# Mixer projections of groups 1 to 7 as 2x2 block products in one fixed order, with the first convolution tap on ScalarE

## Chip, cores and metric

The kernel runs on one core of one Trainium2 chip. The metric is the device time of one execution in microseconds (us), taken as the median of several runs; the profile is of one further execution. All data are float32.

## What is computed

The reference is one decoder block on `x` of 8 sequences with 64 tokens each (512 tokens, 512 channels): a layer norm and a cross-attention (32 heads, 8 key/value heads, 1601 context rows per sequence), a layer norm and a state-space mixer, a layer norm and a routed low-rank expert stage, each added to `x`. The change touches the mixer:

```python
proj = jnp.einsum('bld,pd->blp', hidden_states, in_proj_w)
gate = proj[..., :I]; hbc = proj[..., I:I + CONV_DIM]; dt = proj[..., -H:]
pad = jnp.pad(hbc, ((0, 0), (K - 1, 0), (0, 0)))
conv = conv_bias
for k in range(K):                                   # K = 4 taps
    conv = conv + pad[:, k:k + L, :] * conv_weight[:, k]
xBC = jax.nn.silu(conv)                              # x, B and C
dt_p = jax.nn.softplus(dt + dt_bias); dA = jnp.exp(-dt_p * jnp.exp(A_log))
# scan over tokens: state = state * dA + dt_p * x (outer) B;  y = state . C
y = jnp.moveaxis(ys, 0, 1) + x * D[None, None, :, None]
yg = y.reshape(B, L, G, GROUP_SIZE)
yn = yg * lax.rsqrt(jnp.mean(yg * yg, -1, keepdims=True) + EPS) * norm_weight * silu(gate)
out = jnp.einsum('bli,di->bld', yn, out_proj_w)
```

## The kernel before

The kernel works through the attention first (to about 2268 us of the span), then `mixer_and_routed`, in which the mixer's 64 heads are taken as 8 groups of 8 heads. A group's weights `w_in` make ten row tiles n of 128 rows: n = 0 to 3 are the gates, 4 to 7 the heads' x, 8 is B, 9 is C. Group 0 makes all ten with `project` (L1213 to L1223): four 128x512 matmuls per tile over the contraction of 512, in one PSUM bank `pj`. A float32 matmul leaves two records in the trace, so a tile is 8 records of line L1217. Groups 1 to 7 make tiles 4 to 9 with `project`, and the gates as two pairs of tiles, (0, 1) and (2, 3), with `project_gates` (L1268): a pair of tiles by two halves of 512 channels by two halves of 512 tokens is a 2x2 block product, made with seven half-size products in place of eight.

```python
FIRST = (("a", "L11", "R11"), ("d", "S2", "T2"), ("b", "S1", "T1"), ("c", "S3", "T3"))
SECOND = (("a", "L12", "R21"), ("b", "S4", "R22"), ("c", "L22", "T4"))
```

`first()` makes four of them into the banks `pj_ab` and `pj_cd` (16 records of 128x256, L1279), after which ScalarE copies `a` (L1294) and VectorE makes three sums (L1296 to L1298); `second()` accumulates the other three (12 records) and leaves two more sums (L1305, L1306). The weight sums S1 to S4 come from GpSimd (`weight_sums`, L161 to L164; four instructions per pair, tile `ws`), the token sums T1 to T4 once from VectorE (L1148).

For tiles 4 to 9, `project` goes on with the convolution: the first tap with the bias from PSUM (L1228, VectorE), three more taps (L1234, VectorE, reading `pj` in PSUM and adding to `acc` in SBUF), SiLU (L1240 or L1242, ScalarE). x is also scaled by D (L1246), transposed in 32x32 blocks (L1249, VectorE), and turned by four stores to DRAM (`x_d`) on SyncE's queue and four loads by `load_x` (`dx`).

The other steps, by the names that the change and the trace use: `steps` (L1178, GpSimd, `av`) and `decay` (32 records of L1201 into `seg`, then four Exp into `dec`, L1207) make the decays of a group. `mix` makes C·B (L1317, `pg`), masks it (L1322, `gm`), multiplies it into the decays (L1329, `m`, VectorE) and scales `dx` by dt (L1332, GpSimd). `scan` makes the outputs of a group (128 records of L1347, `py`) and adds them to `y` (L1353, VectorE). `gate` makes the squares (`sq`, ScalarE and GpSimd) and multiplies `y` by the gates (L1369, VectorE). `norm` sums the squares (L1375, `pss`), `project_out` makes the output projection of one of four blocks of 128 tokens (8 records of L1387, `mo`) and adds it to `x` (L1391, VectorE).

A group's decays, scan, gates, norm and outputs run one group late (`old`), between the projections of the group `G`; the decays of the next group (`new`) come a group ahead. The main loop (L1460 on) gives the order in which steps are issued, with `tc.issue_after` at the places where order matters; a list scheduler and the pools settle the rest. The pools are stacked in SBUF in the order in which they are opened: `grpp` (decays, gates, B and C), then `wst` (the weights `w_in` and `w_out`, two buffers each), then `big` and `wk`. `load_in(groups[0])` issues the first group's weights (L1063: four DMAs, two of 1 MB and two of 256 KB) on SyncE's queue while the attention still runs; its address decides which earlier tile has to be free first.

## Time and profile before

| | us |
|---|---|
| median of 3 runs | 2722.01 |
| lowest and highest of them | 2721.52, 2722.79 |
| profiled execution, own time | 2723.19 |
| its span | 2721.5 |
| of the span, TensorE busy | 2703.6 (99%) |
| VectorE, ScalarE, GpSimd busy | 1754.3, 788.8, 802.9 |
| from the mixer's first projection (2272.86) to the end | 448.6 |

The profiled execution's own time is 1.7 us more than its span, and 1.2 us more than the median. In the views, times are microseconds from the start of the span, PE is TensorE's matmuls, PEld its weight loads, DVE VectorE, ACT ScalarE, POOL GpSimd and SP SyncE; "x8" is the number of records in a row, and what stands in brackets is how long the engine had waited and for whom.

### The profile page before, as it was taken

Reading aid. Unit: us, or ns where it says so; the run is one execution under the profiler, and the core shown is the slowest. Engines: PE = TensorE matmul, PEld = TensorE weight load, DVE = VectorE, ACT = ScalarE, POOL = GpSimd, SP = SyncE. Lnnn points to the kernel's source line nnn. Section 1 sums busy time; section 2 is a strip of 40 time slices with the busy share of each in tenths; the row PEclk is TensorE's granted clock in tenths of the full one; section 3 lists DMA queues with packets and bytes.
Section 4 is the critical chain, followed back from the end, with each engine's and each line's share of the span. In section 5 each row is a group of like instructions: output and inputs, shape, how many; then the busy total and the mean of one; then the engine's idle time right before and its main releaser. Section 6 shows DMA issues by size and latency. Waiting matters only on the chain.

```text
span 2721.5 us, 39370 instructions
## 1 busy us (share of the span) xinstructions
PE 2703.6 (99%) x15218; PEld 2002.0 (74%) x15218; DVE 1754.3 (64%) x3071; ACT 788.8 (29%) x1386; POOL 802.9 (30%) x810
## 2 busy tenths in 40 slices
PE   9999999999999999999999999999999999999998
PEld 8777787877788777778787777887777654555555
DVE  5666676576667666766666676667666425676576
ACT  3322222222222232222222222222322102434433
POOL 5323223222222223322333222222333221433321
PEclk9999999999999999999999999999999999999999
DMA  5921322131223213222322132123212370534431
GB/s 174 303 73 48 83 66 62 49 106 44 51 56 90 57 40 79 83 59 42 81 75 61 40 106 50 45 55 92 55 40 71 108 243 12 144 89 107 115 84 41
DMA packets 349716, 222.87 MB, mean 82 GB/s; under 512 B 223932, under 2 KB 309050, under 8 KB 348506
## 3 DMA queue, kind: packets, MB, share of 16 engines
q1 hardware_dynamic: 349530, 220.36, 29.7%
q8 instruction: 121, 1.98, 0.3%
q14 instruction: 65, 0.53, 0.1%
HBM read 189.26 MB, written 31.05 MB: 81 GB/s over the span
## 4 chain that ended last, share of the span: by engine, by line
PE 89%; DVE 6%; DMA 2%; issue 1%; ACT 0%; POOL 0%; SPq 0%; DVEq 0%; ACTq 0%; POOLq 0%
PE pav L647 13%; PE psc L577 13%; PE pv_a L494 6%; PE pv_b L494 6%; PE pk_b L431 6%; PE pk_c L431 6%; PE pv_c L494 6%; PE pk_a L431 6%; PE mo L1387 4%; PE pj L1217 3%; PE pv_d L494 3%; PE pk_d L431 3%; DVE acc L1234 2%; PE psn L463 2%; PE pj_cd L1279 1%; PE pq_ab L241 1%
## 5 line engine op out<-in xcount | busy, mean ns | idle before, releaser
L582 DVE SCALAR_TENSOR_TENSOR attn<-psc,rk,mask_sb 128x256 f32<-128x256 f32 (+1 forms) x832 | 364.5, 476 | 201.2 <-PE psc L577 196.5
L631 POOL TENSOR_TENSOR sm<-attn 128x512 f32<-128x512 f32 x64 | 81.9, 1279 | 1188.3 <-ACT attn L629 1188.3
L647 PE MATMUL pav<-attn,v 128*128 128x256 f32 (+1 forms) x1664 | 380.5, 379 | 0.4 <-ACT o L663 0.4
L577 PE MATMUL psc<-q,kT 128*128 128x256 f32 x1536 | 367.1, 380 | 0.0
L634 POOL TENSOR_TENSOR sm<-sm,attn 128x512 f32<-128x512 f32 x256 | 339.5, 1326 | 29.6 <-DVE attn L625 10.4
L577 PEld LDWEIGHTS psc<-q,kT 128*128 128x128 f32 x1536 | 287.6, 190 | 76.3 <-issue 28.6
L647 PEld LDWEIGHTS pav<-attn,v 128*128 128x128 f32 (+1 forms) x1664 | 311.5, 190 | 43.0 <-issue 1.0
L625 DVE TENSOR_TENSOR attn<-attn,nb 128x1024 f32<-128x1024 f32 x192 | 225.0, 1216 | 52.4 <-ACT nb L622 52.4
L629 ACT ACTIVATE attn<-attn 128x1024 f32<-128x1024 f32 x192 | 203.1, 1058 | 77.7 <-DVE attn L625 71.8
L593 DVE TENSOR_TENSOR mx<-mx,attn 128x512 f32<-128x512 f32 x256 | 212.1, 829 | 2.0
L494 PEld LDWEIGHTS pv_a<-wv,cx 128*128 128x128 f32 x1536 | 191.4, 192 | 9.2 <-issue 2.4
L494 PE MATMUL pv_a<-wv,cx 128*128 128x128 f32 x1536 | 197.9, 275 | 0.0
L431 PE MATMUL pk_a<-cx,wk 128*128 128x417 f32 (+1 forms) x512 | 193.3, 500 | 0.2 <-DVE q_raw L275 0.2
L1217 PE MATMUL pj<-mx_xnT,w_in 128*128 128x512 f32 x416 | 184.8, 597 | 0.0
L442 ACT ACTIVATE ksq<-kT 128x834 f32<-128x834 f32 (+1 forms) x128 | 109.2, 871 | 144.2 <-DVE kT L423 144.2
L1217 PEld LDWEIGHTS pj<-mx_xnT,w_in 128*128 128x128 f32 x416 | 77.1, 190 | 91.9 <-issue 89.3
L431 PEld LDWEIGHTS pk_a<-cx,wk 128*128 128x128 f32 x512 | 97.2, 190 | 45.5 <-issue 21.9
L1387 PE MATMUL mo<-w_out,y 128*128 128x512 f32 x256 | 115.3, 592 | 0.0
L622 ACT COPY nb<-nbs 128x256 f32<-128x256 f32 x64 | 24.1, 376 | 295.6 <-DMA nbs<-max_d 254.6
L421 ACT COPY kT<-pk_a 128x384 f32<-128x384 f32 x64 | 31.5, 493 | 267.4 <-PE pk_a L431 267.4
L694 POOL TENSOR_TENSOR o<-o,f 128x512 f32<-128x512 f32 x31 | 39.7, 1281 | 220.1 <-DMA f<-sums_d 181.9
L1234 DVE SCALAR_TENSOR_TENSOR acc<-pj,small_consts,acc 128x504 f32<-128x504 f32 (+1 forms) x144 | 102.7, 727 | 3.0
(249 smaller groups left out, 4364.1 us busy)
## 6 DMA issues: line engine op xcount, KB each, us to landing
wk<-in_wk SPq DMA_DIRECT2D x32, 512.0 KB
wv<-in_wv SPq DMA_DIRECT2D x32, 512.0 KB
w_in<-in_w_in SPq DMA_DIRECT2D x16, 1024.0 KB
wvs<-wv_s_d SPq DMA_DIRECT2D x28, 512.0 KB
wks<-wk_s_d SPq DMA_DIRECT2D x28, 512.0 KB
cx<-in_ctxT SPq DMA_DIRECT2D x16, 834.0 KB
cx<-in_ctxT SPq DMA_DIRECT2D x16, 768.0 KB
wq<-in_wq SPq DMA_DIRECT2D x16, 512.0 KB
```

The costliest lines, as they stand in the source:

```text
L431: nc.tensor.matmul(ps[:, :w], lhsT=u.wk[l][:, dc, :], rhs=u.cx.r[ch][r][:, dc, :], start=start and dc == 0, stop=dc == 1, skip_group_check ...
L494: nc.tensor.matmul(ps[:, i * HD : (i + 1) * HD], lhsT=u.cx.r[ch][r][:, dc, i * P : (i + 1) * P], rhs=u.wv[l][:, dc, :], start=start and i ...
L577: nc.tensor.matmul(ps[:rows, t - t2, :], lhsT=lhsT, rhs=qh, start=True, stop=True)
L582: nc.vector.scalar_tensor_tensor(out=s.at[:rows, t, :].rearrange("p (h q) -> p h q", h=GQ), in0=ps[:rows, t - t2, :].rearrange("p (h q) -> ...
L593: nc.vector.tensor_tensor(s.mx2, s.mx2, s.at[:, t2 : t2 + 2, :], ALU.max)
L625: nc.vector.tensor_tensor(at[:, k : k + 4, :], at[:, k : k + 4, :], nb.unsqueeze(1).to_broadcast([P, 4, 256]), ALU.add,)
L629: nc.scalar.activation(at[:, k : k + 4, :], at[:, k : k + 4, :], AF.Exp)
L634: nc.gpsimd.tensor_tensor(sm2, sm2, at[:, i : i + 2, :], ALU.add)
L647: nc.tensor.matmul(s.av[:, 0, :], lhsT=u.v[:rows, t, hh, :], rhs=s.at[:rows, t, :], start=t == 0, stop=t == NKT - 1,)
L1217: done = nc.tensor.matmul(pj, lhsT=G.w[:, dc, n, :], rhs=xnT[:, dc, :], start=dc == 0, stop=dc == DC - 1).ins
L1234: taps = nc.vector.scalar_tensor_tensor(out=accb[:, :, k:], in0=pjb[:, :, : S - k], scalar=c.cw[:, ct, KC - 1 - k : KC - k], in1=accb[:, : ...
L1387: last = nc.tensor.matmul(po, lhsT=G.y[:, n, tt * P : (tt + 1) * P], rhs=G.wo[:, n, :], start=n == 0, stop=n == GC - 1,)
```

## The change

All five pairs of tiles, (4, 5), (6, 7), (8, 9), (0, 1) and (2, 3), of groups 1 to 7 go through `project_pair`, the former `project_gates` (names X1, X2, X0, Z0, Z1). The x, B and C pairs are put together in a new SBUF tile `xin`; `convolve` then reads `xin`, with its first tap and bias on ScalarE (Identity with scale and bias) and the other three taps on VectorE. Group 0 keeps `project`, in another order of tiles. The main loop becomes one chain of TensorE steps: each `pe(...)` is issued behind the step before it. PSUM's `pj` has 4 banks in place of 3; the bank `px` is gone, and layer norms and outputs use `y0`, `y1` or `seg`. In SBUF `dec` and `bc` have one buffer in place of two, `p1` and `u2` two in place of one, `ws` four in place of two, and `xin` two.

The diff, without the lines of the old main loop and with smaller hunks left out:

```diff
     def bank(tag, shape, name, bufs=1):
-        return (ps4 if tag in ("pj", "y1") else ps).tile(shape, F32, tag=tag, name=name, bufs=bufs)
+        return (ps4 if tag == "pj" else ps).tile(shape, F32, tag=tag, name=name, bufs=bufs)
...
-        G.l[n] = weight_sums(nc, l, wk.tile([P, 4, 2, P], F32, tag="ws", name="ws"))
+        G.l[n] = weight_sums(nc, l, wk.tile([P, 4, 2, P], F32, tag="ws", name="ws", bufs=4))
...
-                nc, c, small, ps, x, tt, xnT[:, :, tok], tag="px", bufs=2, pbufs=1, copy=nc.scalar.copy
+                nc, c, small, ps, x, tt, xnT[:, :, tok], tag="y0", bufs=2, pbufs=1, copy=nc.scalar.copy
...
-        G.dec = grpp.tile([P, NTT, HPG, S], F32, tag="dec", name="dec")
+        G.dec = grpp.tile([P, NTT, HPG, S], F32, tag="dec", name="dec", bufs=1)
...
-        return last.ins
+        G.exps = last.ins
+        return done.ins
...
-        pj = bank("pj", [P, NT], "pj", 3)
+        pj = bank("pj", [P, NT], "pj", 4)
...
+        return done, convolve(G, n, pj, True), None
+
+    def convolve(G, n, pj, taps):
...
-            G.bc = grpp.tile([P, 2, NT], F32, tag="bc", name="bc")
+            G.bc = grpp.tile([P, 2, NT], F32, tag="bc", name="bc", bufs=1)
...
-        nc.vector.tensor_scalar(
-            acc, pj, c.cw[:, ct, KC - 1 : KC], c.cb[:, ct : ct + 1], op0=ALU.mult, op1=ALU.add
-        )
+        if taps:
+            nc.vector.tensor_scalar(
+                acc, pj, c.cw[:, ct, KC - 1 : KC], c.cb[:, ct : ct + 1], op0=ALU.mult, op1=ALU.add
+            )
+        else:
+            nc.scalar.activation(
+                acc, pj, AF.Identity, scale=c.cw[:, ct, KC - 1 : KC], bias=c.cb[:, ct : ct + 1]
+            )
         accb = acc.rearrange("p (b t) -> p b t", b=B)
         pjb = pj.rearrange("p (b t) -> p b t", b=B)
         for k in range(1, KC):
-            taps = nc.vector.scalar_tensor_tensor(
+            nc.vector.scalar_tensor_tensor(
                 out=accb[:, :, k:], in0=pjb[:, :, : S - k],
                 scalar=c.cw[:, ct, KC - 1 - k : KC - k], in1=accb[:, :, k:],
                 op0=ALU.mult, op1=ALU.add,
...
-    def project_gates(G, n):
+    def project_pair(G, n):
         st, l = Group(), G.l[n]
-        if n == 0:
-            G.sg = grpp.tile([P, GC, NT], F32, tag="sg", name="sg")
-        to = G.sg[:, n : n + 2]
+        gates = n < GC
...
+            if n == 0:
+                G.sg = grpp.tile([P, GC, NT], F32, tag="sg", name="sg")
+            st.to = G.sg[:, n : n + 2] if gates else wk.tile([P, 2, NT], F32, tag="xin", name="xin")
             st.ps = {}
             for pair in ("ab", "cd"):
-                t = bank("pj", [P, 2, HT], f"pj_{pair}", 3)
+                t = bank("pj", [P, 2, HT], f"pj_{pair}", 4)
                 st.ps[pair[0]], st.ps[pair[1]] = t[:, 0, :], t[:, 1, :]
             for k, lhs, rhs in FIRST:
...
-            p1 = wk.tile([P, HT], F32, tag="p1", name="p1", bufs=1)
+            p1 = wk.tile([P, HT], F32, tag="p1", name="p1")
             nc.scalar.copy(p1, st.ps["a"])
-            st.u2 = wk.tile([P, HT], F32, tag="u2", name="u2", bufs=1)
+            st.u2 = wk.tile([P, HT], F32, tag="u2", name="u2")
             nc.vector.tensor_tensor(st.u2, p1, st.ps["d"], ALU.add)
             nc.vector.tensor_tensor(p1, st.u2, st.ps["b"], ALU.add)
-            nc.vector.tensor_tensor(to[:, 1, HT:], p1, st.ps["c"], ALU.add)
+            nc.vector.tensor_tensor(st.to[:, 1, HT:], p1, st.ps["c"], ALU.add)
             return last
         def second():
+            to = st.to
             for k, lhs, rhs in SECOND:
                 last = product(k, lhs, rhs, False, True)
-            nc.scalar.activation(to[:, 0, :HT], st.ps["a"], AF.Silu)
+            if gates:
+                nc.scalar.activation(to[:, 0, :HT], st.ps["a"], AF.Silu)
+            else:
+                nc.scalar.copy(to[:, 0, :HT], st.ps["a"])
             nc.vector.tensor_tensor(to[:, 0, HT:], st.u2, st.ps["b"], ALU.add)
             nc.vector.tensor_tensor(to[:, 1, :HT], st.u2, st.ps["c"], ALU.add)
-            nc.scalar.activation(to[:, 0, HT:], to[:, 0, HT:], AF.Silu)
-            return last, nc.scalar.activation(to[:, 1, :], to[:, 1, :], AF.Silu).ins
-
-        return first, second
+            if gates:
+                nc.scalar.activation(to[:, 0, HT:], to[:, 0, HT:], AF.Silu)
+                st.silu = nc.scalar.activation(to[:, 1, :], to[:, 1, :], AF.Silu).ins
+            return last
+
+        def convolved():
+            for k in range(2):
+                st.silu = convolve(G, n + k, st.to[:, k, :], False)
+
+        st.first, st.second, st.convolved = first, second, convolved
+        return st
...
-        po = bank(tag, [P, D], "mo", 3 if tag == "pj" else 1)
+        po = bank(tag, [P, D], "mo", 4 if tag == "pj" else 1)
...
-        layernorm_T(nc, c, small, ps, x, tt, xnT, tag="px", bufs=2, pbufs=1, copy=nc.scalar.copy)
+        layernorm_T(nc, c, small, ps, x, tt, xnT, tag="seg", bufs=2, pbufs=2, copy=nc.scalar.copy)
...
-    last = decay(g0)
+    decay(g0)
+    last = g0.exps
+    chain = Group()
+
+    def pe(what, *of):
+        with tc.issue_after(chain.last):
+            chain.last = what(*of)
+
+    def begin(new, g):
+        load_out(groups[g])
+        if new:
+            load_in(new)
+        else:
+            load_routed()
+
     for g in range(G2):
         G, old = groups[g], groups[g - 1] if g else None
         new = groups[g + 1] if g + 1 < G2 else None
...
+        begin(new, g)
+        if not old:
+            with tc.issue_after(last):
+                for n in (8, 9, 4, 0, 5, 1, 6, 2, 7, 3):
+                    chain.last, silu, _ = project(G, n)
+            load_x(G)
+            token_sums()
+            for n in (4, 6, 8, 0):
+                sums_in(new, n)
+            pe(mix, G)
+            for tt in range(NTT):
+                steps(new, tt)
+            with tc.issue_after(silu):
+                table = load_ln_exp(nc).ins
+            with tc.issue_after(table):
+                pe(decay, new)
+                weigh_out(G)
+            last = new.exps
+            continue
+        X1, X2, X0, Z0, Z1 = (project_pair(G, n) if n in G.l else None for n in (4, 6, 8, 0, 2))
+        with tc.issue_after(last):
+            pe(X1.first)
+            pe(X2.first)
+            pe(X1.second)
+            sums_in(G, 2)
+            Z1 = project_pair(G, 2)
+            X1.convolved()
+            pe(scan, old, 0)
+            pe(scan, old, 1)
+            pe(X2.second)
+            if new:
+                sums_in(new, 4)
+            for tt in range(NTT):
+                gate(old, tt)
+            if not new:
+                X2.convolved()
+                load_x(G)
+            pe(X0.first)
+            with tc.issue_after(X1.silu):
+                table = load_ln_exp(nc).ins
+            pe(Z0.first)
+            pe(X0.second)
+            if new:
+                sums_in(new, 6)
+            with tc.issue_after(table):
+                pe(norm, old, range(NTT))
+        with tc.issue_after(old.normed):
+            if new:
+                X2.convolved()
+                load_x(G)
+            pe(Z0.second)
+            if new:
+                sums_in(new, 8)
+            X0.convolved()
+            pe(project_out, old, 0, "y0")
+            if not new:
+                pe(mix, G)
+            pe(Z1.first)
+            pe(project_out, old, 1, "y1")
+            if new:
                 for tt in range(NTT):
                     steps(new, tt)
...
             else:
...
+                pe(scan, G, 0)
+                pe(scan, G, 1)
+                for tt in range(NTT):
+                    squares(G, tt)
+            pe(Z1.second)
             if new:
...
+                sums_in(new, 0)
+                pe(mix, G)
+            pe(project_out, old, 2, "y0")
+            pe(project_out, old, 3, "y1")
+            if new:
+                with tc.issue_after(Z1.silu), tc.issue_after(X0.silu):
+                    table = load_ln_exp(nc).ins
+                with tc.issue_after(table):
+                    pe(decay, new)
+                last = new.exps
+            else:
+                last = Z1.silu
             weigh_out(G)
...
```

## The prediction

> **What bounds the kernel now.** I read the page first, then TensorE's waits in the mixer, then one steady group, VectorE's rows, and the start of the mixer.
>
> ```profile
> PE 2703.6 (99%) x15218; PEld 2002.0 (74%) x15218; DVE 1754.3 (64%) x3071; ACT 788.8 (29%) x1386; POOL 802.9 (30%) x810
> PE 89%; DVE 6%; DMA 2%; issue 1%; ACT 0%; POOL 0%; SPq 0%; DVEq 0%; ACTq 0%; POOLq 0%
> PE pj_cd L1279 <- DVE acc L1234: 3.8, 7, 1.0
> ```
>
> TensorE is the bound: busy for 99% of the span and 89% of the chain that ended last. The third line, from the waits after 2260 us, is its largest wait in the mixer: 3.8 us over seven groups. So matmul time removed is gained, and any new wait in front of a matmul is paid in full.
>
> The timeline of TensorE in a steady group gives the prices (start, us, engine, line, records):
>
> ```profile
> 2355.58 1.03 PE L1279 MATMUL pj_ab<-mx_xnT,w_in 128*128 128x256 f32 x4
> 2356.44 1.03 PE L1279 MATMUL pj_cd<-mx_xs,ws 128*128 128x256 f32 x4
> 2357.30 1.03 PE L1279 MATMUL pj_ab<-mx_xs,ws 128*128 128x256 f32 x4
> 2358.17 1.03 PE L1279 MATMUL pj_cd<-mx_xs,ws 128*128 128x256 f32 x4
> 2359.03 3.60 PE L1387 MATMUL mo<-w_out,y 128*128 128x512 f32 x8
> ...
> 2376.12 14.00 PE L1217 MATMUL pj<-mx_xnT,w_in 128*128 128x512 f32 x32
> 2389.96 0.95 PE L1375 MATMUL pss<-ones,s 128*128 128x1 f32 x8
> ```
>
> From start to start, 32 straight records take 13.84 us (0.4325 each) and 16 block records 3.45 us (0.2156 each). A group repeats every 53.2 us (2343.40 to 2396.60).
>
> **Removed: 21 straight pairs.** A straight pair is 16 x 0.4325 = 6.92 us, a block pair 28 x 0.2156 = 6.04 us: 0.88 us saved. Three pairs in each of seven groups give 2.64 us a group, 18.5 us in all. If the old waits (0.9 us in the group shown) go too, 3.5 us a group.
>
> **Added on VectorE and moved there.** Per group six first taps of 0.80 us go to ScalarE (6 x about 0.61; it has 22 us of work in 53), and 15 sums of 0.42 us come (five per pair): 36 us become 37.5, still under TensorE's 50. ScalarE's 0.61 us goes ahead of each pair's taps; I put it into the 0.5 us of handover below. But their place matters, and so does the source of the 18 taps that stay: PSUM before, SBUF after. The rows, as shortest/median/longest ns:
>
> ```profile
> L1234 DVE SCALAR_TENSOR_TENSOR acc<-pj,small_consts,acc x122: 681/732/745, 2325.5 to 2662.6; 128x496 f32<-128x496 f32 x41, 128x488 f32<-128x488 f32 x41, 128x504 f32<-128x504 f32 x40
> L1369 DVE TENSOR_TENSOR y<-y,sg x28: 680/776/1257, 2337.1 to 2654.0; 128x512 f32<-128x512 f32 x28
> L298 DVE SCALAR_TENSOR_TENSOR q_st<-q_raw,qw,qrsb x32: 739/747/1225, 42.8 to 136.1; 128x512 f32<-128x512 f32 x32
> ```
>
> With one input in PSUM (L1234) the duration hardly varies; with both in SBUF (L1369, L298) it reaches 1.2 us, with means of 0.88 and 0.81. GpSimd's load grows from 19 to 28 us a group (12 more weight sums of 0.727). I bound a tap by 0.73 and 0.88 and take 0.80, next to L298, the same kind of instruction.
>
> The Trainium skill, "SBUF — State Buffer", Who interferes with whom, says that a VectorE instruction with two SBUF inputs contends with a GpSimd instruction that reads SBUF, one waiting until the other is through; the spread of L1369 agrees. If each tap waited half of a 0.73 us weight sum during the half of the time in which GpSimd works, it would cost 0.2 us more, 3.3 us a group, and the forecast would rise by some 15 to 20 us.
>
> **Steady groups.** The chain gives two places where TensorE's next step needs VectorE. First, from the end of X1.second to X0.second. In the built order VectorE has: the rest of X1's sums (2 x 0.46), its six taps (6 x 0.64, the pitch of taps on alternate tiles), four additions of `py` (4 x 0.63), two transposes (2 x 0.62), X2's sums (0.9), four products with the gates (2.08 + 1.28), X0's first sums (0.9): 13.7 us. TensorE meanwhile has scan 2.02, X2.second 2.59, X0.first 3.45, Z0.first 3.45: 11.5 us; Z0 also needs X2's banks. That is 2.2 us short, with 0.5 for ScalarE's copies in between 2.7. Second, up to Z1.second, VectorE has the convolutions of X2 and X0 (12 taps, 7.7 us), two transposes, the sums of Z0 and two additions to `x`, some 13.5 us, beside 12.9 us of TensorE: about 0.6, and decay's second half waits some 0.3 for y0 and y1. At the old tap price the waits are 3.6 against the 3.5 gained, so nothing remains; at 0.80, with about 15 taps in those stretches, 1.0 us is lost per group (up to 2.4 at 0.88; 0.4 gained if the two places overlap better). Groups 2 to 6: +5 us (-2 to +12). The stores and loads of x (four per tile on SyncE, and `load_x`) move by less than half a group; their consumer, the scan, comes a group later, some 25 us: nothing, and at most the 4.3 us of four dx products if that cover went. `dec` with one buffer makes the Exp of the next decays wait for the four products `m` (2.5 us); outputs 2 and 3 (6.9 us) stand between: nothing, or up to 2.5 us a group without them. The layer norms and the routing change banks, not work: within 0.5 us either way, taken as nothing.
>
> **Group 1.** In the built order GpSimd gets `sums_in(G, 2)` ahead of the four dx products that scan(0) needs, and its buffer is only free after X1.second. TensorE comes to the scan right after that, so it waits 4 x 0.727 + 1.07 less the handover, 3.6 us, and then 3 x (1.07 - 0.53) = 1.6 us for the other three: +5.2 us (4 to 6). The rest of the group gains 1.5 us (1 to 3).
>
> **Last group.** X2's six taps and two transposes (5.2 us) stand before X0's sums, so X0.second waits not 2.7 but about 6.5 us; and `mix` stands right after the first output, where B and C still need six taps and SiLU: about 3.8 us. Less 1.7 of waits before and the 2.64: +6.0, with slower taps +6.5 (3 to 9).
>
> **Start of the mixer.** The diff does not show this; the built program does. `grpp` shrinks by 12 KB per partition, so `w_in` of group 0 lies elsewhere, and its load now waits for the last matmul of the attention's output projection, behind that one's own loads on SyncE. Before:
>
> ```profile
> 2192.18 0.39 SPq L1063 DMA_DIRECT2D w_in<-in_w_in  x1
> 2196.39 1.57 SPq L1063 DMA_DIRECT2D w_in<-in_w_in  x3
> ...
> 2266.63 1.02 PE L793 MATMUL po_d<-spare,o_last 128*128 128x512 f32 x2
> ...
> 2272.86 13.10 PE L1217 MATMUL pj<-mx_xnT,w_in 128*128 128x512 f32 x30
> 2284.82 0.42 DVE L1130 SCALAR_TENSOR_TENSOR a<-dt,a_sb 128x256 f32<-128x256 f32 x1
> 2285.88 0.65 PE L1154 MATMUL psw<-a,ident 128*64 128x256 f32 x4
> 2291.29 0.66 PE L1201 MATMUL seg<-av,past 64*64 64x256 f32 x8 [0.34 <-POOL av L1178]
> 2291.88 9.71 PE L1217 MATMUL pj<-mx_xnT,w_in 128*128 128x512 f32 x22
> ```
>
> After, the load starts at 2267.7; tile 8 is the third DMA, behind 2 MB. At the 0.35 MB/us that the DMA view shows around 2200 us, it lands at about 2276 to 2278 rather than being there at 2272.9. The scheduler puts 2 matmuls of `project` in front of `psw`, where 15 stood (30 records). `psw` waits for `a`; without convolutions in between VectorE gets there at 2281.8 (2276.8 + 0.28 + 0.41 + 0.42 + 1.74 + 4 x 0.42 and gaps), and the decays end 6.07 us after `psw` as before: 2287.9 in place of 2291.9. But then 36 matmuls remain, not 23: -4.0 + 13 x 0.865 = +7.2 us, and 0.7 for the next decays, which wait for `seg`: +8 (5 to 10).
>
> In this start TensorE would idle twice for about 4 us. The clock dips in one row of the trace only, the tail with its many waits (us, PE busy, ..., clock 0.92):
>
> ```profile
> 2710.00:2722.00 12.00, 5.15 (x26) 2.92 (x24) 4.25 (x14) 1.32 (x4) 0.00 (x0) 0.92 0.18 66
> ```
>
> I add nothing for it. The Trainium skill, "TensorE: Matmul & The Clock Gate", Part 1, has the clock fall to half after an idle window of some 3.4 us; such a window's work at half rate would add an estimated 1.7 us per gap, which speaks against the change.
>
> **Sum.** 8 + 5.2 - 1.5 + 5 + 6.5 = +23 us on the profiled execution's 2723.2, so 2746.4; that execution is 1.2 us above the median: 2745.
>
> **Rivals.**
> (a) Faster: VectorE keeps up, because taps on alternate tiles keep the 0.64 us pitch and its queue gets its slack from the four banks of `pj`. Then TensorE stays gapless: -18.5 and -3.8 of old waits, against +8 at the start: -14; with group 1's scan too, -9. 2708 to 2713. For it: VectorE's sum, 37.5 of 50 us. Against: its queue is in order and the two stretches ask 13.7 of 11.5 us.
> (b) The taps are much slower, 0.95 us or more, as L1369's longest of 1.257 allow: 15 x 0.15 more in each of seven groups, +16 on the forecast, 2761.
> (c) The change doesn't do what it says in the sense that gain and waits cancel: early load despite the new address, dx in time, groups at -0.4: -2 - 1.5 + 6, near 2724. It decides only if both start terms vanish.
>
> **How the numbers follow.** A measurement of this kernel can tell about 0.2% (5.4 us) from no change. Forecast 0.66, with the bounds above (+6 to +38: 2728 to 2760); (b) 0.12; (a) 0.17; (c) 0.05. The range from 2718 to 2762 leaves out (a) and the far end of (b). Faster 0.17, same 0.05, slower 0.78; the slower cases' own range is 2728 to 2762.
>
> **What would show it.** Right: TensorE's waits on VectorE in every group at X0.second or Z0.first, about 3 to 4 us; the L1063 load of group 0 issued after 2267; py in group 1 waiting on dx or ws; a mean tap of about 0.80; block pairs at 6.04. Wrong: groups at a period under 50.5 us (then (a)), taps above 0.9 (then (b)), or `w_in` of group 0 landing before 2272.

## Result, and the profile after

The changed kernel takes 2766.91 us (median of 4 runs, 2766.52 to 2767.49), the kernel before 2722.4 us beside it: a ratio of 1.0164, with a 95% interval of 1.0146 to 1.0182. It is slower by 44.5 us, where +23 was forecast. The direction and each of the places named were right, the sizes were not, and the time lies above the range. The profiled execution took 2767.49 us, 0.6 us over the median; its span is 2765.8, 44.3 us more than before.

The page of after, its busy times and the chain:

```profile
PE 2707.4 (98%) x15470; PEld 2062.0 (75%) x15470; DVE 1787.1 (65%) x3134; ACT 830.8 (30%) x1473; POOL 889.9 (32%) x894
PE 89%; DVE 7%; ACT 1%; DMA 1%; POOL 1%; issue 1%; SPq 0%; DVEq 0%; ACTq 0%; POOLq 0%
```

TensorE's busy time is 3.8 us longer although matmul time was removed: part of it runs at a lower clock. GpSimd has 87 us more: 84 more weight sums, 61 us at 0.73 us each, and slower instructions. TensorE's waits from 2255 us to the end (total, times, longest) are where 3.8 us stood before:

```profile
PE pj_ab L1287 <- DVE p L1308: 19.4, 11, 7.1
PE pj_ab L1287 <- DVE xin L1320: 12.3, 6, 2.2
PE py L1370 <- POOL dx L1354: 4.8, 4, 3.9
PE pg L1339 <- ACT bc L1250: 4.2, 1, 4.2
PE pj L1218 <- DMA w_in<-in_w_in: 3.6, 1, 3.6
```

They make 44 us, as much as the whole loss, and leave no room for the matmul time saved, so something else must be longer too. Lines have moved: `project` is now L1218, the block products L1287, the copy of `a` L1305, the first sums L1307 to L1309, the second sums L1320 and L1321, the first tap L1238, the other taps L1244, the gate products L1393, `mo` L1412. Each wait is placed by TensorE's timeline (start, us, engine, line, records, and the wait ahead): the start of the mixer, group 1's scan, group 2's Z0.first, X0.second and Z1.second, and the last group.

```profile
2275.43 3.78 PE L1218 MATMUL pj<-mx_xnT,w_in 128*128 128x512 f32 x4 [3.61 <-DMA w_in<-in_w_in]
...
2335.17 1.13 PE L1370 MATMUL py<-m,dx 64*64 64x64 f32 x32 [3.93 <-POOL dx L1354]
...
2340.51 2.07 PE L1287 MATMUL pj_ab<-mx_xnT,w_in 128*128 128x256 f32 x4
...
2403.38 1.13 PE L1287 MATMUL pj_ab<-mx_xnT,w_in 128*128 128x256 f32 x4 [2.20 <-DVE xin L1320]
...
2408.89 1.10 PE L1287 MATMUL pj_ab<-mx_xnT,w_in 128*128 128x256 f32 x4 [1.79 <-DVE p L1308]
...
2426.86 1.10 PE L1287 MATMUL pj_ab<-mx_xnT,w_in 128*128 128x256 f32 x4 [1.33 <-DVE p L1308]
...
2694.14 2.05 PE L1287 MATMUL pj_ab<-mx_xnT,w_in 128*128 128x256 f32 x4 [7.14 <-DVE p L1308]
2695.98 1.91 PE L1287 MATMUL pj_ab<-mx_xnT,ws 128*128 128x256 f32 x4
...
2710.78 2.08 PE L1339 MATMUL pg<-bc 128*128 128x128 f32 x8 [4.21 <-ACT bc L1250]
```

Two things are to be seen. The long waits stand where the prediction put them. And the rows behind the long ones last about twice as long: a row of four block records is 1.03 us elsewhere, 2.05, 1.91 and 1.91 here; the `pg` row 1.05 elsewhere, 2.08 here. Below this is called half pitch, and the usual spacing full pitch. In the stretch from 2340 to 2346 us the granted clock is 0.62, in 2682 to 2740 it is 0.85, and in 2383 to 2439, with only the shorter waits, 1.00.

By stages, on the two spans (a group's stage starts with the first row of its steps on TensorE: the products of X1 in after; in before a product of `project`, or for groups 2 to 6 the row of decays in front of it):

| stage | before | after | difference | predicted |
|---|---|---|---|---|
| end of the attention | 2267.65 | 2266.44 | -1.2 | 0 |
| from there to group 1 | 47.05 | 55.04 | +8.0 | +8 |
| group 1 | 53.88 | 61.67 | +7.8 | +3.7 |
| groups 2 to 6 | 5 x 53.2 | 5 x 56.16 | +14.8 | +5 |
| last group and tail | 86.9 | 101.8 | +14.9 | +6.5 |
| sum | | | +44.3 | +23 |

VectorE's taps from SBUF, and what ran on VectorE and on GpSimd around 2394 us (the second row from VectorE's timeline, the third and fourth from GpSimd's):

```profile
L1244 DVE SCALAR_TENSOR_TENSOR acc<-xin,small_consts,acc x126: 711/742/1508, 2332.1 to 2708.6; 128x504 f32<-128x504 f32 x42, 128x496 f32<-128x496 f32 x42, 128x488 f32<-128x488 f32 x42
2393.79 5.62 DVE L1244 SCALAR_TENSOR_TENSOR acc<-xin,small_consts,acc 128x504 f32<-128x504 f32 x6 [0.42 <-ACT acc L1238]
2397.74 1.15 POOL L163 TENSOR_TENSOR ws<-w_in 128x256 f32<-128x256 f32 x1
2398.85 1.15 POOL L162 TENSOR_TENSOR ws<-ws,w_in 128x256 f32<-128x256 f32 x1
```

The median tap is 0.742 us, near the 0.732 it was from PSUM, but the longest are twice that: by the groups view the mean of one is 0.93 us, and the 126 keep VectorE busy for 110.9 us (where one overlaps the next, the time counts once). The six taps that X0.second needs took 5.62 us. The weight sums beside them took 1.15 us instead of 0.73.

### The profile page after: what moved, and what is told of

It reads as the page before. It is cut to its first block, busy times and chain, and to the rows that moved or that the text cites. A ratio compares the mean times of both kernels' runs of the same rounds, so it can differ in the third digit from the quotient of the medians.

```text
span 2765.8 us, 40173 instructions
## 1 busy us (share of the span) xinstructions
PE 2707.4 (98%) x15470; PEld 2062.0 (75%) x15470; DVE 1787.1 (65%) x3134; ACT 830.8 (30%) x1473; POOL 889.9 (32%) x894
## 4 chain that ended last, share of the span: by engine, by line
PE 89%; DVE 7%; ACT 1%; DMA 1%; POOL 1%; issue 1%; SPq 0%; DVEq 0%; ACTq 0%; POOLq 0%
PE pav L647 13%; PE psc L577 12%; PE pv_a L494 6%; PE pv_b L494 6%; PE pk_b L431 6%; PE pv_c L494 6%; PE pk_c L431 6%; PE pk_a L431 6%; DVE acc L1244 3%; PE pv_d L494 3%; PE pj_ab L1287 3%; PE pk_d L431 3%; PE mo L1412 2%; PE pq_ab L241 2%; PE psn L463 2%; PE pj_cd L1287 2%
## 5 line engine op out<-in xcount | busy, mean ns | idle before, releaser
L1244 DVE SCALAR_TENSOR_TENSOR acc<-xin,small_consts,acc 128x504 f32<-128x504 f32 (+2 forms) x126 | 110.9, 932 | 12.7 <-ACT acc L1238 12.6
L1412 PE MATMUL mo<-w_out,y 128*128 128x512 f32 x256 | 114.2, 592 | 0.0
L1287 PE MATMUL pj_ab<-mx_xnT,w_in 128*128 128x256 f32 x280 | 79.3, 408 | 31.9 <-DVE p L1308 19.4
L431 PE MATMUL pk_b<-cx,wks 128*128 128x384 f32 (+1 forms) x256 | 97.3, 502 | 0.4
```

The source lines that it names most:

```text
L431: nc.tensor.matmul(ps[:, :w], lhsT=u.wk[l][:, dc, :], rhs=u.cx.r[ch][r][:, dc, :], start=start and dc == 0, stop=dc == 1, skip_group_check ...
L1244: nc.vector.scalar_tensor_tensor(out=accb[:, :, k:], in0=pjb[:, :, : S - k], scalar=c.cw[:, ct, KC - 1 - k : KC - k], in1=accb[:, :, k:], ...
L1287: last = nc.tensor.matmul(st.ps[k], lhsT=l[lhs][:, dc, :], rhs=blocks[rhs][:, dc, :], start=start and dc == 0, stop=stop and dc == 1, skip ...
L1412: last = nc.tensor.matmul(po, lhsT=G.y[:, n, tt * P : (tt + 1) * P], rhs=G.wo[:, n, :], start=n == 0, stop=n == GC - 1,)
```

## Experiments

The theory after the result: (T1) the loss in the steady groups comes mostly from VectorE's taps, slowed by GpSimd's weight sums, on the path to X0.second and Z0.first; (T2) beyond each long wait the matmuls run at a lower clock, which adds to it; (T3) the start, group 1 and the last group each have the wait that the prediction named. The rivals: that the block products are dearer on TensorE than their rows say, that VectorE's total work is the bound, or that the tap count alone makes the waits. All differences below are against 2766.91 us; the kernel before stayed within 2722.1 to 2722.6 us beside them.

**x_load: the early load alone.** The pools are opened in another order, so that the first group's `w_in` lies elsewhere.

```diff
     grpp = ctx.enter_context(tc.tile_pool(name="mx_grp", bufs=2))
-    wst = ctx.enter_context(tc.tile_pool(name="mx_w", bufs=2))
     big = ctx.enter_context(tc.tile_pool(name="mx_big", bufs=1))
+    wst = ctx.enter_context(tc.tile_pool(name="mx_w", bufs=2))
```

> The changed kernel with the pools in another order in SBUF (big ahead of wst), so that the first group's w_in lies where nothing of the end of the attention lies: its load is issued before the last block of the output projection again, and the built order has 15 matmuls of project in front of psw, not 2. Nothing else is changed. Theory (the late load costs the start): the stretch from the end of the attention to X1.first of group 1 shrinks by 7 to 9 us, from 55.0 to about 47, no row at half pitch there, time about 2759. Rival (the start is slow because of group 0's new order of tiles and the decay of group 1 behind pg, whatever the load): at most 2 us, time 2765 or more.

Measured: 2758.83 us (2756.94 to 2759.68), -8.1 us. The first group's four loads of L1063 are issued from 2225.07 to 2233 us on SyncE (from 2266.47 in after, 2192.18 to 2198 in before), the first 30 records of `project` run from 2271.44, ahead of `psw`, without a wait, and group 1 begins at 2314.37 instead of 2321.48. From the end of the attention (2265.82) to group 1 it takes 48.55 us, where after has 55.04 and before 47.05. So 6.5 of the 8.0 us at the start are the effect of an address, as predicted. The other 1.5 us stay: the row of decays at its end takes 3.15 us in x_load as in after (at 2318.40), and 1.96 in before.

**x_nows: without the weight sums.** The sums S1 to S4 are left out (each is a copy of L21 by name), so that GpSimd doesn't run them.

```diff
-        G.l[n] = weight_sums(nc, l, wk.tile([P, 4, 2, P], F32, tag="ws", name="ws", bufs=4))
+        G.l[n] = dict(l, S1=l["L21"], S2=l["L21"], S3=l["L21"], S4=l["L21"])
```

> The changed kernel without the weight sums: S1 to S4 are replaced by a block of the weights itself, so that GpSimd loses 16 of its 20 weight-sum instructions per group and more; matmuls, sums, taps and their order stay. Theory P (taps with two SBUF inputs are held up by GpSimd's reads): the mean tap falls from 880 ns to about 750, the three waits of a steady group from 5.3 to about 3.5 us, its period from 56.2 to about 54, and with the last group and group 1's scan the time falls by 15 to 20 us, to about 2750. Rival O (taps are slow by themselves, or the waits come from VectorE's order alone): the mean tap stays at 0.85 us or more, and only group 1's scan gains, 3 to 6 us: 2762.

Measured: 2750.64 us (2748.42 to 2755.0), -16.3 us. The taps in the groups view of VectorE:

```profile
L1244 DVE SCALAR_TENSOR_TENSOR acc<-xin,small_consts,acc 128x504 f32<-128x504 f32 (+2 forms) x126 | 88.2, 755 | 12.6 <-ACT acc L1238 12.6
```

A mean of 0.755 us where it was 0.93; the six taps ahead of X0.second take 4.02 us where they took 5.62. Two of the five steady groups take 53.4 us (2400.50 to 2453.89 is such a period), with waits of 0.60 at Z0.first and 2.20 at X0.second instead of 5.3 in three places. The other three take 55.0 to 55.1, because the rows behind the same wait run at half pitch:

```profile
2400.50 1.97 PE L1287 MATMUL pj_ab<-mx_xnT,w_in 128*128 128x256 f32 x8 [2.19 <-DVE p L1308]
...
2453.89 3.41 PE L1287 MATMUL pj_ab<-mx_xnT,w_in 128*128 128x256 f32 x8 [2.20 <-DVE p L1308]
```

By stages, the five steady groups give back 8.9 us (1.8 each in the mean, 2.8 where no row is at half pitch), and group 1 gives back 8.0. Only the first of these can be put down to the contention: in group 1 the sums that stood ahead of the dx products on GpSimd are gone as well. In the steady groups a shorter GpSimd queue could help by itself, through the squares; VectorE's idle time in front of the gate products, where that would show, falls only from 10.6 to 8.1 us over all seven groups. So T1 holds for the larger part of the 14.8 us that the steady groups lost: 8.9, of which a small share may be the queue's. The waits of the last group (7.1 and 4.4 us) stay, so they have another cause.

**x_warm: matmuls without a use in the last group's waits.** Seven 128x512 matmuls ahead of X0.second and four ahead of `mix`; their result is not read.

```diff
+    def warm(n):
+        t = bank("seg", [P, NT], "warm", 2)
+        for _ in range(n):
+            done = nc.tensor.matmul(t, lhsT=c.ones, rhs=xnT[:, 0, :], start=True, stop=True)
+        return done.ins
...
+            if not new:
+                pe(warm, 7)
             pe(X0.second)
...
+                pe(warm, 4)
                 pe(mix, G)
```

> The changed kernel with 11 more matmuls that nobody reads, in the last group only: 7 of 128x512 between Z0.first and X0.second, where TensorE waited 7.1 us, and 4 in front of mix, where it waited 4.2 us. Theory C (an idle TensorE is clocked down, and the rows after the wait run at half pitch): the records after both waits come back to full pitch, 2.6 us at X0.second and about 3 us at mix and Z1.first: the time falls by 5 us, to 2762, although work was added. Rival (those rows are slow for their own reasons, weight loads or banks): nothing gained, 2767 or up to 2 us more.

Measured: 2761.43 us (2761.22 to 2761.81), -5.5 us from added work. TensorE's timeline at the place that had 2.05 and 1.91:

```profile
2694.04 1.10 PE L1287 MATMUL pj_ab<-mx_xnT,w_in 128*128 128x256 f32 x4 [1.14 <-DVE p L1308]
2694.97 1.03 PE L1287 MATMUL pj_ab<-mx_xnT,ws 128*128 128x256 f32 x4
```

X0.second starts at the same time (2694.04 for 2694.14), and the rows behind it are at full pitch. T2 holds here: the two long waits of the last group cost 5.5 us in clock beyond their own length.

**x_last: the last group's steps as in the others.** X2's convolution stands behind the norm, and `mix` behind Z1.first.

```diff
-            if not new:
-                X2.convolved()
-                load_x(G)
             pe(X0.first)
...
-            if new:
-                X2.convolved()
-                load_x(G)
+            X2.convolved()
+            load_x(G)
...
+            pe(Z1.first)
             if not new:
                 pe(mix, G)
-            pe(Z1.first)
```

> The changed kernel with the last group's convolutions and mix where the other groups have them: X2's taps after norm, mix behind Z1.first. Theory (X2's taps in front of X0's sums make the 7.1 us wait): the wait at X0.second falls to about 1.8 us and no row runs at half pitch behind it, -7 us; mix waits less, -3 us; the scan of the last group may now wait for dx, up to +4: time 2757 to 2761. Rival (the transfers of x through DRAM set the last group): the wait moves to the scan in full, 2766.

Measured: 2761.55 us (2761.32 to 2763.23), -5.4 us. The wait at X0.second falls from 7.14 to 2.19 us as predicted from the order of VectorE's queue, yet the rows behind it are still 1.72, 1.91 and 1.30; `pg` still waits 3.40 us, and its row and the output product behind it are slow (2.08 and 5.63 us where 1.05 and 3.60 are usual). So the lower clock can follow a wait of 2.2 us too. The second wait is for SiLU of B and C (`bc`), which stands behind their own taps, and it shrinks by only 0.8 us when X2's taps are moved.

**x_g1: group 1's last weight sums behind the dx products on GpSimd.**

```diff
-            sums_in(G, 2)
+            with tc.issue_after(old.scaled):
+                sums_in(G, 2)
```

> The changed kernel with one order added: the weight sums of group 1's last pair come on GpSimd behind the four dx products of group 0's scan, not ahead of them. Theory (group 1's scan waits for GpSimd's queue): the 3.9 us wait and the four 0.3 us waits at py go, and with them the half pitch of the rows that follow (2.1 us): time falls by 6 to 8 us, to 2760. Rival (dx has not landed by then anyway, or Z1's weight sums are now late): 0 to 3 us, 2764 or more.

Measured: 2762.34 us (2761.44 to 2763.87), -4.6 us, less than expected. TensorE's timeline shows why: the scan's waits are gone but for 0.74 us, and one of 2.90 appears at Z0.first, with slow rows behind it.

```profile
2343.69 1.13 PE L1287 MATMUL pj_ab<-mx_xnT,w_in 128*128 128x256 f32 x4 [2.90 <-DVE xin L1320]
2344.66 1.85 PE L1287 MATMUL pj_cd<-mx_xs,ws 128*128 128x256 f32 x4
```

**x_notaps: two of the three VectorE taps left out** in groups 1 to 7.

```diff
-        for k in range(1, KC):
+        for k in range(1, KC if taps else 2):
```

> The changed kernel with two of the three VectorE taps left out for x, B and C of groups 1 to 7 (24 us less of VectorE in every... 12 taps a group, some 11 us). Theory P (the taps' price alone makes the waits): all waits on VectorE go and a steady group takes TensorE's own 50 us, 6 less: with the last group and group 1 some 45 us less, 2722. Theory O (the order counts as much: X0's sums stand behind the scan's additions and the gates whatever the taps cost): one wait of about 3 us stays at X0.second, steady groups take about 53 us, the last group's 7 and 4 us waits stay for the most part: 2740 to 2744.

Measured: 2750.65 us (2749.84 to 2752.65), -16.3 us. That takes away 84 of the 126 taps and 67 us of VectorE's busy time (1787.1 to 1720.5), and yet a steady group still takes 54.6 us (2376.86 to 2431.50) with one wait of 2.9 us at X0.second. VectorE itself waits there:

```profile
2401.53 0.69 DVE L1393 TENSOR_TENSOR y<-y,sg 128x512 f32<-128x512 f32 x1 [3.75 <-ACT sq L1383]
```

The last gate product waits for the squares that ScalarE makes of `y`, which it overwrites, and X0's sums stand behind it in VectorE's queue. So VectorE's amount of work isn't the bound, and the number of taps alone doesn't make the waits: with fewer taps, a second chain takes their place. The time lies 7 us above the second theory's range.

**x_sq: four buffers for the squares, nothing else.** The squares on ScalarE wait for GpSimd's sums of the squares before (`s`, 1.31 us at 2406.61 in after), because they share two buffers.

```diff
-        sq = grpp.tile([P, GC, P], F32, tag="sq", name="sq")
+        sq = grpp.tile([P, GC, P], F32, tag="sq", name="sq", bufs=4)
```

> The changed kernel with four buffers in place of two for the squares (tile sq), nothing else: TensorE's, VectorE's and GpSimd's orders are the same, ScalarE's too but for one table load placed behind the squares. In the changed kernel the third and fourth square wait for GpSimd's sums s, which stand behind the weight sums; ScalarE's copy of X0's bank a (p1) stands behind them, and X0's sums and X0.second behind that copy. Theory S (the chain weight sums on GpSimd, squares on ScalarE, copy, sums sets the wait at X0.second): that wait of 1.8 us in groups 2 to 6 and part of the last group's go: 1.0 to 1.8 us a group, 5 to 9 us in all, 2758 to 2762. Rival (VectorE is late there by its own taps whatever ScalarE does): 0 to 2 us.

Measured: 2761.17 us (2759.7 to 2762.65), -5.7 us. X0.second's wait in a steady group falls from 1.79 to 0.95 us, and the period from 56.16 to 55.3 (55.8 in one of the five, with rows at half pitch). The chain from GpSimd's `s` through ScalarE's squares and its copy of `a` to X0's sums was the end of that wait, by 0.84 us a group; what holds the other 0.95 isn't shown by this run.

**x_onepair: the kernel before, with one pair of x tiles, (6, 7), as a block product** in its own order, with its own pools and start. The core of the diff against the kernel before (`project_pair` and `convolve` are those of the change; `ws` has three buffers, `p1` and `u2` two, and `xin` one):

```diff
-                        done, silu, taps = project(G, n)
+                        if G.g and n == 6:
+                            pair = project_pair(G, n)
+                            done = pair.first()
+                        elif G.g and n == 7:
+                            with tc.issue_after(done):
+                                done = pair.second()
+                            pair.convolved()
+                            silu, taps = pair.silu, pair.taps
+                        else:
+                            done, silu, taps = project(G, n)
```

> The kernel before, with its own order, pools and start, and only tiles 6 and 7 of groups 1 to 7 made as a block pair with the first tap on ScalarE (one more set of weight sums per group on GpSimd). TensorE has 0.88 us less per group, 6.2 in all. Theory (a block pair needs its first sums from VectorE in the middle of the pair, and VectorE's queue in order is not there in time): about 2 us of wait at second() of that pair and as much at the gates' pair behind it, in every group: slower than before, 2736 to 2745. Rival (one pair fits into the slack of VectorE; only all three at once are too much): 6 us faster, 2716 to 2719.

Measured: 2735.46 us (2734.38 to 2737.57), a ratio of 1.0047 (1.0031 to 1.0064) to before: slower by 13 us, although by the pitches of the rows (0.88 us a pair) TensorE has 6.2 us less to do. From TensorE's waits (L1330 is the new pair, L1288 the gates' pairs):

```profile
PE pj_ab L1330 <- DVE p L1351: 7.4, 7, 2.0
PE pj_cd L1288 <- DVE acc L1243: 3.0, 1, 3.0
```

With 2.8 and 2.2 us more at two other places, the waits are 15 us, 11.6 more than in before; the rows behind the longest one (2.96 us in the last group) take 3.65 us instead of 1.99. In a steady group the waits are 2.0 us, half of what was expected, where 0.4 stood before; the period grows by 1.1 (53.2 to 54.3), so 0.5 of the 0.88 us arrives. The taps took 0.748 us in the mean, so it isn't slow taps that make these waits. So a single x pair already loses to waits, without the late load, `mix` or the new order.

**x_order: the steps in another order, with weight sums still on GpSimd.** With the early load and dx first, one product of the scan ahead of X1.second, the squares ahead of X2.second, and X1's convolution behind X0.first.

```diff
+                pe(X2.first)
+                pe(scan, old, 0)
+                pe(X1.second)
+                with tc.issue_after(old.scaled):
+                    sums_in(G, 2)
+                Z1 = project_pair(G, 2)
+                pe(scan, old, 1)
+                for tt in range(NTT):
+                    squares(old, tt)
+                pe(X2.second)
...
+                pe(X0.first)
+                X1.convolved()
...
```

> The changed kernel's operations, all five pairs, with another order and other pools: big ahead of wst (early load), scan 0 between X2.first and X1.second, X1's taps behind X0.first and the first two gate products, weight sums of group 1's last pair behind dx, mix before outputs 2 and 3, output 2 ahead of Z1.second so that VectorE has more TensorE time to work in, and the last group with its taps behind the first sums. Theory (the loss is order and place, not the products): the early load gives 8 us, dx 4, the last group 10 or more, and steady groups come from 56.2 to about 52: 2718 to 2726, level with the kernel before or a little faster. Rival (taps with two SBUF inputs and 38 us of VectorE per group can't be hidden in any order): steady groups at 54 or more, 2735 or more.

Measured: 2745.3 us (2743.07 to 2745.47), a ratio of 1.0082 (1.0067 to 1.0097). Missed by some 20 us. The waits on `p` remain:

```profile
PE pj_ab L1287 <- DVE p L1308: 22.3, 8, 3.3
```

The steady groups take 55.6 or 57.0 us, as the rival had it (54 or more). The taps still take 0.924 us in the mean, and the gate products, which also have two SBUF inputs, 1.085 us where they took 0.83. This order moves the contention; it doesn't take it away. That no order could is not shown.

**x_dve: the weight sums on VectorE.** Twenty sums of 0.41 us per group go to VectorE, at the end of a group's steps, so that GpSimd no longer reads weights beside the taps; with the early load, and the squares and the norm ahead of X0.second.

```diff
-        G.l[n] = weight_sums(nc, l, wk.tile([P, 4, 2, P], F32, tag="ws", name="ws", bufs=4))
+        G.l[n] = weight_sums(nc, l, wk.tile([P, 4, 2, P], F32, tag="ws", name="ws", bufs=5), nc.vector.tensor_tensor)
...
+                pe(project_out, old, 2, "y0")
+                for n in (4, 6, 8, 0, 2):
+                    sums_in(new, n)
+                X2.convolved()
...
```

> All five block pairs stay and all results are computed. Three edits on the changed kernel: the weight sums of all pairs run on VectorE at the end of each group's step order, so that GpSimd keeps only its products and squares of the outputs; the load of group 0's w_in is early again, as in x_load (8 us); and the steps of a group stand in another order, with the squares, then the normalization, ahead of X0's first sums, and half of the gate products behind X0.second. Theory (the taps are slow because GpSimd's weight sums read SBUF beside them, and the block pairs lose what they gain where a wait of over 2 us is followed by matmuls at half pitch): taps fall to 0.75 to 0.80 us as in x_nows, no group has a wait of over 2 us, no rows at half pitch stand in the steady groups, and a steady group takes about 52.5 us: 2718 to 2730. Rival 1: the 20 sums of weights cost VectorE some 7 to 12 us more per group, which brings waits of 2 us and more in front of the second halves: 2735 or more. Rival 2: the block pairs themselves are dearer on TensorE than their rows say, so that also without waits the groups stay at 53.5 us or more.

Measured: 2726.78 us (2724.72 to 2729.18, 11 runs), a ratio of 1.0016 (1.0007 to 1.0025), -40 us. VectorE has more to do than in any other kernel here (1814.5 us of the span), and the taps take 0.779 us; a steady group takes 52.76 us with one wait of 0.96. That is what T1 expects and rival 1 excludes. (The order of steps isn't quite that of x_order, so the 18.5 us between the two aren't the weight sums' alone.) Rival 2 is half right: without waits a group still has 51.8 us where the pitches gave 50. One part of it can be seen in TensorE's timeline, in front of the decays:

```profile
2371.30 1.05 PE L1339 MATMUL pg<-bc 128*128 128x128 f32 x8
2372.29 3.06 PE L1201 MATMUL seg<-av,past 64*64 64x256 f32 x32
```

The row of decays is 3.06 us long where it was 2.00 in after: the reading put to the test in x_dve2 is that half of them need a bank of `seg` that VectorE is still reading `pg` from. A wait inside a row isn't shown as one. The other loss is at the start: the weight sums of group 1 ran on VectorE from 2254.64, between the rows of the attention's last layer norm, and the first projection began at 2276.14 instead of 2271.44.

**x_dve2: both taken away.** Group 1's weight sums on GpSimd, and `mix` ahead of the last output product.

```diff
-        ... bufs=5), nc.vector.tensor_tensor)
+        ... bufs=5), nc.vector.tensor_tensor if G.g > 1 else nc.gpsimd.tensor_tensor)
...
-                pe(project_out, old, 3, "y1")
-                for tt in range(NTT):
-                    steps(new, tt)
                 X0.convolved()
                 pe(mix, G)
+                for tt in range(NTT):
+                    steps(new, tt)
+                pe(project_out, old, 3, "y1")
```

> x_dve with two edits, all results computed. (1) Group 1's weight sums go back to GpSimd: in x_dve VectorE ran them from 2254.64 us, between the rows of the layer norm that ends the attention, so that a transpose of it waited 3.1 us on TensorE and the first projection began at 2276.14 where x_load has 2271.44; expected -4.7 us. (2) The products pg (C with B) go ahead of the last output product, not behind it: in x_dve the decays' matmuls stand right behind pg and need the bank that VectorE is still reading, and their row is 3.06 us long where it is 2.00 in x_load; expected -1.05 us in each of six groups. Theory (TensorE's sum plus its waits is the whole time): 11 us less than x_dve, 2714 to 2719, and so below the kernel before. Rival: VectorE's time, not TensorE's, is what a group now lasts, since the sums fill it; then what is taken away in one place comes back as a wait at the next second half, and it stays within 3 us of x_dve's 2727 less the 4.7 of the start: 2720 to 2725.

Measured: 2719.12 us (2717.53 to 2721.45, 11 runs), a ratio of 0.9989 (0.998 to 0.9998): level with the kernel before by the bound of 0.2%, on the faster side, 48 us below the changed kernel with the same five block pairs. The steady group is 51.70 us, and its wait and decays are

```profile
2386.82 1.13 PE L1287 MATMUL pj_ab<-mx_xnT,w_in 128*128 128x256 f32 x4 [0.95 <-DVE xin L1320]
...
2417.24 2.00 PE L1201 MATMUL seg<-av,past 64*64 64x256 f32 x32
```

The start gave 4.2 us and each steady group 1.06, as the theory has it. Group 1 gave 3.55, which wasn't forecast: its wait at Z0.first fell from 2.17 to 1.34 us, and the rows behind it, at half pitch in x_dve, are at full pitch. Against that, group 6 takes 53.4 us, because its decays now wait 1.09 us for VectorE's addition to `x`, and the last group and the tail took back 3.7 us (88.3 to 92.0). So the time lies at the edge between the theory's range and the rival's. In the last group the sums of the squares wait, and the block products behind them run slowly, though only waits of 0.18 and 1.35 us are shown:

```profile
2651.41 0.59 PE L1398 MATMUL pss<-ones,s 128*128 128x1 f32 x2 [1.35 <-DVE u L1307]
2651.86 2.05 PE L1287 MATMUL pj_ab<-mx_xnT,w_in 128*128 128x256 f32 x4
```

## Why the prediction was too low

Measured are 21 us more than forecast: 4.1 in group 1, 9.8 in the steady groups and 8.4 in the last group, less 1.2 at the end of the attention. The direction and the places came out right. Three terms of the sum failed. The clock behind the waits was put at nothing and cost 8.2 us. The taps, priced at 0.80 us or 1.0 us a group, took 0.93, and up to 2.5 us of waits a group hang on that. And the gain of 3.5 us a group was 2.4. Stage by stage:

**The start: right, step by step.** The load went out at 2266.47 (2267.7 predicted), the first projection ran at 2275.43 (2276 to 2278), `psw` at 2280.40 (2281.8), the first decays ended at 2286.41 (2287.9), all some 1.2 us early because the attention ended so much earlier. The stage is 8.0 us longer for +8 predicted. The split was a little off: the load is 6.5 us of it by x_load (7.2 predicted), and 1.5 are left for the decays and the rest (0.7 predicted).

**Group 1: the wait right, two terms too small.** The scan waited 3.93 us (3.6). Its other three rows come 1.43 us apart, since a dx product took 1.47 us here and not 1.07: 3 x 0.9 = 2.7 us for 1.6. The clock, which the prediction left out, costs 2.7 us more: 0.6 in the scan's last row and 2.1 in the three block rows behind it (4.70 us from 2340.51 to 2345.21 for 2.6). Less the 1.5 that was predicted as gained, 3.9 + 2.7 + 2.7 - 1.5 is the +7.8 measured, for +3.7; the 1.5 is what the sum leaves over, not measured by itself. x_g1 gave back only 4.6 us, because Z0.first then waits 2.9.

**Steady groups: the gain too large, the taps too cheap.** Forecast were +1.0 us a group: 3.6 of waits, 1.0 more by slower taps, and -3.5 gained. Measured are +3.0. In groups 2 and 4, which have no row at half pitch, it splits like this:
- The gain was 2.4 and not 3.5. TensorE's time without its waits fell from 52.78 us (53.2 less 0.42) to 50.83 (56.16 less 5.33), by 1.95 and not 2.64. Part of the difference is that the first row behind another kind of step has a pitch of 0.94 to 0.97 us instead of 0.865 (2403.38 to 2404.35 in after's timeline). And the old wait was put at 0.9 from one group, where 0.42 stands in the period measured here and 3.8 us over seven groups are 0.54.
- The taps' price was the term most mis-sized of these: 0.80 us, with 0.88 as the upper bound, from the means of L298 and L1369; it was 0.93. The waits without contention were 2.8 us (x_nows: 0.60 and 2.20), less than the 3.6 forecast, which hid a part of the error; the sums beside the taps add 2.5, not 1.0. The rows of before held both kinds of duration, near 0.75 and up to 1.25 us; a mean from another stretch can't say how many there will be of each, when the change itself more than doubles GpSimd's weight sums.
- The 0.5 us for ScalarE's part was too small. The first tap took 0.800 us, not 0.61 (before's L1246, with a scale per partition, already took 0.72), and the copy of `a` stands in ScalarE's queue behind squares that wait for GpSimd's `s`: 0.84 us a group by x_sq. x_notaps shows that this chain holds a wait of 2.9 us by itself once the taps are out of the way.

The Trainium skill, "SBUF — State Buffer", Who interferes with whom, has a VectorE instruction with two SBUF inputs and a GpSimd instruction that reads SBUF exclude each other. The prediction quoted it with an estimate of 15 to 20 us over the forecast, and set it aside. Taps at 0.755 us without the weight sums and 0.93 with them agree with the rule. The estimate was 3.3 us a group; x_nows gave back 1.8 a group in the mean, and 2.8 where no row was at half pitch.

**Last group: the waits right, the clock missing.** X0.second waited 7.14 us (6.5 predicted) and `pg` 4.21 (3.8). Not forecast were 1.27 us at Z0.first (2683.27), 0.7 less gained by the pairs, and 5.5 us of half pitch (x_warm): 0.6 + 0.4 + 1.3 + 0.7 + 5.5 = 8.5 over the +6.5, where +14.9 was measured.

**The clock: "I add nothing for it" was wrong,** though the tail's row with 0.92 stood in the prediction. It costs 5.5 us in the last group and 2.7 in group 1. At the start four records took 3.78 us instead of 1.98 and it cost nothing, because `psw` waited 1.19 us for VectorE all the same. The Trainium skill, "TensorE: Matmul & The Clock Gate", Part 1, puts the loss behind an idle window of some 3.4 us. Behind the waits of 3.6, 3.9, 4.2 and 7.1 us the rows agree. But half pitch also followed waits of 2.19 us (x_last), 2.9 us (x_notaps, x_g1), and the short products that sum the squares, with waits of 0.18 and 1.35 us between them (x_dve2); there the measurement decides. In x_dve waits of 0.16 and 1.36 us between the same short products were followed by full pitch. In after the wait of 2.2 us at Z0.first was followed by full pitch in groups 2 and 4 and by half pitch in groups 3, 5 and 6; from group 3:

```profile
2460.51 1.76 PE L1287 MATMUL pj_cd<-mx_xs,ws 128*128 128x256 f32 x4
...
2465.06 1.10 PE L1287 MATMUL pj_ab<-mx_xnT,w_in 128*128 128x256 f32 x4
```

What decides between them stays open. There it costs nothing: X0.second starts 5.51 us after Z0.first in groups 2 to 6 alike, since it waits for VectorE's sums, and the slow rows only fill that wait (1.79 us in group 2, none in group 3). All five groups last 56.15 to 56.19 us.

**Rivals.** (a), a gapless TensorE, was put at 2708 to 2713. x_dve2, with another order and the sums elsewhere, comes near it in the steady groups, and to 2719: the pairs give 2.0 us a group instead of 2.64, 0.96 us of waits are left, and the last group isn't gapless. (b) was nearest: its taps of 0.95 us or more came close to the 0.93 measured. That it is only 6 us short is partly luck, since it had no clock either and priced the taps' excess alike in all seven groups. (c) fell with the start.

## What to carry to other kernels

A saving of matmul time counts only as far as the engines that feed the next matmul keep their distance: here some 14 us of matmuls were saved (7 x 1.95), and the waits of the five steady groups alone grew from 2.2 to 21.5 us; with the early load, another order of steps and the helper sums on the busier VectorE, the same products took 48 us less. When a change turns PSUM operands into SBUF operands and gives GpSimd more SBUF reads, price the instruction at its contended duration, in proportion to the other engine's busy time, not at a mean from elsewhere in the trace. Allow for a wait of 2.2 us or more in front of TensorE to be dearer than its length, by 1.4 to 2.9 us in the cases here, unless the next step would have waited anyway; and ask of every pool that changes its size which prefetch now lies behind which last reader: here one went out 74 us later.

## What the runs showed of the hardware

- VectorE's taps (128x488 to 128x504) with both inputs in SBUF: 0.755 us in the mean without GpSimd's weight sums, 0.93 with them; GpSimd's weight sum beside them 1.15 us for 0.73. Both sides lose.
- TensorE at half pitch behind waits as short as 2.2 us, in some places and not in others; 11 matmuls without a use gave back 5.5 us.
- ScalarE's Identity with a scale and a bias per partition, 128x512 from SBUF to SBUF: 0.800 us (0.797 to 0.815), where its Copy with a scale per partition takes 0.71 and its SiLU 0.63 at the same size.
